# Attention outputs turned by VectorE and exchanged through DRAM instead of turned by TensorE, with other places for the adjacency loads

## The chip, the core and the metric

The kernel runs on one core of a Trainium2 chip. A core has five engines that each work through their own list of instructions in order: TensorE (PE; its weight loads are listed apart as PEld), VectorE (DVE), ScalarE (ACT), GpSimd (POOL) and SyncE (SP), which here only issues DMA transfers. An engine that meets an instruction whose semaphore is not yet up stands still, and so does all that is behind it in that list. The metric is the device time of one launch in microseconds (us), lower is better.

## The reference, cut to what matters

There are 16 graphs of 1024 nodes with 256 features, each with a symmetric 0/1 adjacency matrix with ones on its diagonal.

```python
h = relu(layernorm(x))
# layer 0: 8 heads of 32, queries = keys = values
normed = layernorm(h) * gamma1 + beta1
scores = einsum('bhqd,bhkd->bhqk', qkv, qkv) / sqrt(32)     # qkv: normed cut into heads
attn   = softmax(where(adj > 0, scores, -inf))
h      = h + einsum('bhqk,bhkd->bhqd', attn, qkv)
x      = x + h + gelu((layernorm(h)*gamma2 + beta2) @ W1 + b1) @ W2 + b2
# layer 1: one head over all 256 features
f = relu(layernorm(x)); hh = f @ W
e = leaky_relu(hh @ a_1 (per key and per query with a_2) + (hh @ a_12) @ hh.T, 0.2)
x = x + elu(f @ W_1 + softmax(where(adj > 0, e, -9e15)) @ f @ W_2)
```

All of it is float32. `adj` comes as int32, 4 MB for each graph. Because the queries of layer 0 are also its keys, the scores are symmetric, and so are the masked weights as long as `adj` is.

## The kernel before, in words

A graph (`b`, 0 to 15) is worked on in two halves, and two graphs are always in work at once: `attention(b)`, layer 0's attention of graph b, runs interleaved with `rest(b - 1)`, which is all that comes after the attention for the graph before it (the MLP with the groups `ph` and `po`, and layer 1 with `puT`, `pg`, `lg`, `pf`, `pa`).

**Order.** The program is written out by a small planner in Python, so that the order of instructions on every engine is fixed when the program is built. Six generators (`stream_a` for attention, `stream_b` for the rest, `stream_p` for the norms between them, `stream_c` for the prologue of the next graph, `stream_m` for the adjacency, `stream_s` for set-up) yield places on an axis on which graph b's attention covers b to b+1; the one with the lowest place goes next. A second clock counts estimated microseconds: `defer(us, f)` queues f until that clock has moved on by `us`. `turns` is a list of small TensorE transposes that `make_turns` puts between units. So a place such as b - 0.43 moves loads along the whole axis, and a `defer` of 2.0 instead of 3.0 moves one step by a fraction of a unit.

**Attention.** The heads are taken in groups of four (`g` = 0, 1), the queries in halves of 512 (`qh`), the keys in tiles of 128 (`kt`). A unit is one (qh, g, kt). It computes scores `s` on TensorE (line 1010), adds the mask on VectorE (L1023, `e<-s,mk`), takes Exp on ScalarE with the row sums (L1030), and one unit later multiplies with the values, `o<-e,va` (L1125), into one PSUM bank, the pool `pso` with a single buffer. From graph 1 on, symmetry is used: in the units with qh = 0, `keys` runs 4, 0, 5, 1, 6, 2, 7, 3, and for kt of 4 and more, `mirror` turns the weights in 32x32 blocks on VectorE (L1046), writes them to a DRAM scratch (`blocks`, L1053, four DMAs a unit) and adds up their columns on GpSimd (L1059, sent through `rows` and `gather`). In the second half (qh = 1) the lower key tiles are not computed again: `fetch(k)` loads them back from `blocks` into one half of the tile `em` (L1093), and `weigh_mirrored(k)` multiplies them (L1107), k from 0 to 15, two for each unit. Fetch k+2 may begin only when product k has been read. A graph thus has 16 units with qh = 0 and 8 with qh = 1.

**The end of a group.** When the last key tile of a (g, qh) is in, four groups a graph, `weigh` copies `o` (4 heads x 32 features on the partitions, 512 queries along them) to SBUF on VectorE (`os`, L1134). `close` puts `finish` into `turns`: four TensorE transposes to PSUM (`ptos`, L976) bring the queries onto the partitions, VectorE multiplies with the inverse row sums `rl` (`ot`, L978), and GpSimd adds the product to `h` (L982). `invert` makes `rl` from the row sums on VectorE. `prepare(b, st, c)` then takes layer norm statistics of `h` for chunk c of 256 rows; `rest` waits in its planning loop until `finished[b, 1]` is 2 before it prepares chunk 2.

**Adjacency.** `turn_masks(b, qh)` loads four tiles of 128 rows as int32 halves (`adj`, L587, two buffers), converts them on VectorE to fp8 (`mq`, L594, one buffer), and turns them with transposing DMAs into `mk` (L917, five buffers). `compare_masks` checks the symmetry: GpSimd subtracts `mk` and `mq` (`odd`, L932), and ScalarE sums the squares of the difference into a column of `uneven` (L941). If that or another condition fails at the end, a general path, not run here, computes everything again.

All bulk transfers go through SP's one list. Six lines show the two places where it meets the change:

```python
if n == NG * NT - 1:            # n counts the units of a graph, NG * NT = 16
    defer(2.0, lambda: fetch(0))
    defer(2.2, lambda: fetch(1))
...
if n == NG * NT + 1:
    gather(1)
```

Of the kernel before, what the change touches and what calls it, by code (L numbers as in the profile page):

```python
# [495 lines left out]
def fast_path(  # L496
# [427 lines left out]
    def compare_masks(b, qh, st):  # L924

        for half in range(qh + 1):
            for i in range(TPH):
                kt = qh * TPH + i
                odd = tmpp.tile([P, QW], BF16, tag="w1", bufs=6, name=f"odd_{b}_{qh}_{half}_{i}")
                key = st[half][:, kt // 2, :, kt % 2]  # L930
                query = st["mq", qh][:, i, half * QW : (half + 1) * QW]
                nc.gpsimd.tensor_tensor(  # L932
                    odd.rearrange("p (u v x) -> p u v x", u=2, v=2),
                    key.rearrange("p (u v x) -> p u v x", u=2, v=2),
                    query.rearrange("p (u x v) -> p u v x", u=2, v=2),
                    op=ALU.subtract,
                )
                n = (b * 3 + qh + half) * TPH + i
                defer(
                    3.0,  # L940
                    lambda odd=odd, n=n: nc.scalar.activation(odd, odd, AF.Square, accum_out=uneven[:, n : n + 1]),  # L941
                )
                yield
        if (b, qh) == (B - 1, NQH - 1):
            defer(
                4.0,
                lambda: nc.vector.tensor_reduce(
                    seen[:, 4:5], uneven, axis=mybir.AxisListType.X, op=ALU.add
                ),
            )  # L950
# [14 lines left out]
    scored = []  # L965

    finished = {}

    def finish(b, qh, g, rl, ready, os):
        h = hs[b]  # L970
        run_deferred(ready)
        finished[b, qh] = finished.get((b, qh), 0) + 1
        clock[0] += 0.5
        pt = ps_tile([P, TPH, P], f"ptos_{b}_{g}_{qh}")
        for t in range(TPH):
            nc.tensor.transpose(pt[:, t, :], os[:, t * P : (t + 1) * P], ident)  # L976
        ot = tmpp.tile([P, TPH, GH, HD], F32, tag="w2", bufs=4, name=f"ot_{b}_{g}_{qh}")
        nc.vector.tensor_mul(  # L978
            ot, pt.rearrange("p t (j d) -> p t j d", d=HD), rl.unsqueeze(3).to_broadcast([P, TPH, GH, HD])
        )  # L980
        ho = h[qh][:, :, g * P : (g + 1) * P]
        nc.gpsimd.tensor_add(ho, ho, ot.rearrange("p t j d -> p t (j d)"))  # L982

    def attention(b, st):
        va, kT = st["va"], st["kT"]
# [54 lines left out]
        def mirror(g, kt, es):  # L1040
# [17 lines left out]
            def add_up():  # L1058
                add = lambda out, p, q: nc.gpsimd.tensor_tensor(out, p, q, op=ALU.add)  # L1059
                part = denp.tile([P, TPH * GH, GH, 8], F32, tag="part", bufs=1, name=f"part_{b}_{g}_{kt}")  # L1060
                add(part, x[:, :, :, 0:8], x[:, :, :, 8:16])
                add(part, part, x[:, :, :, 16:24])
                add(part, part, x[:, :, :, 24:32])
                add(part[:, :, :, :4], part[:, :, :, :4], part[:, :, :, 4:])
                add(part[:, :, :, :2], part[:, :, :, :2], part[:, :, :, 2:4])
                row = denp.tile([P, GH, TPH, GH], F32, tag="row", name=f"row_{b}_{g}_{kt}")
                add(
                    row.rearrange("p a t h -> p t a h"),
                    part[:, :, :, 0].rearrange("p (t a) h -> p t a h", a=GH),
                    part[:, :, :, 1].rearrange("p (t a) h -> p t a h", a=GH),  # L1070
                )
# [48 lines left out]
        def weigh(qh, g, kt, es, first, last):  # L1120
            if first and not (mirrored and qh == 1):
                acc[g, qh] = pso.tile([P, QW], F32, tag="o", name=f"o_{b}_{g}_{qh}")
            o = acc[g, qh]
            for j in range(GH):
                nc.tensor.matmul(  # L1125
                    o[j * HD : (j + 1) * HD, :],
                    va[:, kt, (g * GH + j) * HD : (g * GH + j + 1) * HD],
                    es[j // 2][:, j % 2, :],
                    start=first and not (mirrored and qh == 1),
                    stop=last,  # L1130
                )
            if last:
                c = os[g, qh] = tmpp.tile([P, QW], F32, tag="w2", bufs=4, name=f"os_{b}_{g}_{qh}")
                nc.vector.tensor_copy(c, o)  # L1134
                if qh == NQH - 1:
                    close(qh, g)

        def close(qh, g):
            turns.append((1, lambda: finish(b, qh, g, *rl[g, qh], os[g, qh])))

        def invert(qh, g):
            r = smallp.tile([P, TPH, GH], F32, tag="rl", name=f"rl_{b}_{g}_{qh}")

            def f():
                if mirrored and qh == 0:
# [8 lines left out]
                )  # L1154
                nc.vector.reciprocal(r, r)

            rl[g, qh] = r, defer(2.5 if mirrored and qh == 0 else 2.5, f)

        keys = list(range(NT))
        if mirrored:  # L1160
# [5 lines left out]
        for n, u in enumerate(units):  # L1166
# [8 lines left out]
            if not mirrored:  # L1175
                if qh == NQH - 1 and kt % TPH == TPH - 1:
                    invert(kt // TPH, g)
                    if kt < NT - 1:
                        close(kt // TPH, g)
                yield 1.0  # L1180
                continue
            if qh == 0:
                if kt >= TPH:
                    mirror(g, kt, es)
                if n == NG * NT - 1:
                    defer(2.0, lambda: fetch(0))
                    defer(2.2, lambda: fetch(1))
                if n == NT + 1:
                    gather(0)
                if n == NT + 3:  # L1190
                    invert(0, 0)
                    close(0, 0)
                yield 1.0
                continue
            if n == NG * NT + 1:
                gather(1)
            if n == NG * NT + 3:
                invert(0, 1)
                close(0, 1)
# [46 lines left out]
    def rest(b, st, tails):  # L1246
# [476 lines left out]
```

## Time and profile before

| | |
|---|---|
| runs | 3390.57, 3390.76, 3401.56 us; median 3390.76 us |
| profiled execution | 3397.68 us; the profile's span in it 3395.4 us |
| mean granted TensorE clock | 0.988 of full |
| TensorE busy | 3239.8 us, 95% of the span |
| VectorE / ScalarE / GpSimd busy | 2584.0 (76%) / 2205.2 (65%) / 1515.3 us (45%) |
| `ptos` transposes, L976 | x256, 42.0 us |
| `os` copy, L1134; `ot` product, L978 | x64, 43.6 us; x64, 43.9 us |
| `odd` squares, L941 | x192, 119.9 us, with 37.0 us of accumulator reads |
| DMA through SP's queue | 397.14 MB, 48.0% of 16 engines' span |

A row of the groups names the line, the engine, the operation, the tile written and those read, the shape and the count; then the busy time and the mean of one, and after the bar the idle time of that engine just before such instructions with the names of those that ended it. A row of the waits says which engine and line waited for whom: us in total, times, the longest. A row of the windows gives, for a stretch of the span, busy us and instruction count of each engine, then the granted TensorE clock, the mean busy share of the DMA engines and GB/s. SPq is SP's list of issues.

### The profile page before, as it was taken

The page shows a single profiled execution, that of the slowest core. Times are in us where ns is not written, and L with a number is a line of the kernel's source. Part 1 is how long each engine was busy: PE and PEld are TensorE (multiplying, and loading weights), DVE is VectorE, ACT ScalarE, POOL GpSimd, SP SyncE. Part 2 cuts the span into 40 slices and gives each one's busy share as a digit, 9 for nine tenths or more (in the row PEclk, how much of TensorE's full clock was granted, in tenths as well). Part 3 has the DMA queues.
Part 4 walks back from the last instruction along what each step waited for, and adds up shares of the span by engine and source line. Part 5 has one row for each costly group of instructions (what it writes and reads, how often), then busy time and mean ns, then how long its engine had stood idle before and what let it go on. Part 6 is the DMA issues. An engine that isn't in the chain of part 4 may idle for free. (4 is left out here: it accounts for less than half of the span.)

```text
span 3395.4 us, 114970 instructions
## 1 busy us (share of the span) xinstructions
PE 3239.8 (95%) x48866; PEld 1600.2 (47%) x48866; DVE 2584.0 (76%) x4881; ACT 2205.2 (65%) x5384; POOL 1515.3 (45%) x1757
## 2 busy tenths in 40 slices
PE   6899999999999999999999999999999999999998
PEld 2244445444444444444444454444544444444477
DVE  5677787777888778787787887778877787877734
ACT  6875756758567585665757567585675856758553
POOL 3563543635436364453635436354362543636120
PEclk9999999999999999999999999999999999999999
DMA  5256454454654455555455544645445464444410
GB/s 136 69 112 141 114 134 128 102 150 116 141 131 109 131 120 133 132 119 128 109 147 123 135 121 110 150 115 136 126 104 141 114 144 127 109 130 113 119 36 14
DMA packets 741161, 404.82 MB, mean 119 GB/s; under 512 B 173217, under 2 KB 699937, under 8 KB 740641
## 3 DMA queue, kind: packets, MB, share of 16 engines
q1 hardware_dynamic: 740352, 397.14, 48.0%
q8 instruction: 386, 6.32, 0.8%
q14 instruction: 135, 1.10, 0.1%
q10 hardware_dynamic: 288, 0.26, 0.0%
HBM read 233.97 MB, written 146.54 MB: 112 GB/s over the span
## 5 line engine op out<-in xcount | busy, mean ns | idle before, releaser
L1030 ACT ACTIVATE e<-e 128x512 f32<-128x512 f32 x1504 | 929.5, 620 | 496.6 <-DVE e L1023 493.2
L1023 DVE TENSOR_TENSOR e<-s,mk 128x1024 f32<-128x1024 f32 x752 | 885.2, 1217 | 197.5 <-PE s L1010 182.8
L574 PE MATMUL lg<-fT,uT 128*32 128x256 f32 x7680 | 471.1, 392 | 0.0
L574 PE MATMUL ph<-yT,w 128*32 128x256 f32 x7808 | 443.3, 380 | 7.0 <-DVE yT L1292 7.0
L574 PE MATMUL pa<-gw,e 128*32 128x258 f32 x7584 | 446.1, 380 | 0.0
L1010 PE MATMUL s<-kT 32*64 32x512 f32 x6272 | 442.1, 614 | 0.9 <-DVE e L1023 0.9
L574 PE MATMUL po<-w,hid 128*32 128x256 f32 x7680 | 434.4, 379 | 0.0
L1125 PE MATMUL o<-e,va 128*32 128x512 f32 x3136 | 422.5, 606 | 0.4 <-ACT e L1030 0.4
L574 PEld LDWEIGHTS lg<-fT,uT 128*32 128x32 f32 x7680 | 255.8, 113 | 211.0 <-issue 48.4
L574 PEld LDWEIGHTS ph<-yT,w 128*32 128x32 f32 x7808 | 250.5, 110 | 210.4 <-issue 29.0
L1046 DVE STREAM_TRANSPOSE x<-e 128x1024 f32<-128x1024 f32 x240 | 293.7, 1239 | 73.0 <-ACT e L1030 44.4
L574 PEld LDWEIGHTS po<-w,hid 128*32 128x32 f32 x7680 | 250.0, 110 | 202.8 <-issue 45.2
L574 PEld LDWEIGHTS pa<-gw,e 128*32 128x32 f32 x7584 | 246.0, 110 | 185.5 <-issue 22.1
L1409 DVE SCALAR_TENSOR_TENSOR e<-lg,gw,mk 128x256 f32<-128x256 f32 x512 | 223.5, 478 | 125.9 <-PE lg L574 114.9
L1059 POOL TENSOR_TENSOR part<-part,x 128x512 f32<-128x512 f32 x240 | 310.3, 1293 | 18.8
L1415 ACT ACTIVATE e<-e,shift 128x512 f32<-128x512 f32 x256 | 183.5, 717 | 159.8 <-DVE e L1414 149.0
L1030 ACT ACTIVATION_READ_ACCUMULATOR e<-e 128x1 f32 x1504 | 283.4, 188 | 0.0
L1059 POOL TENSOR_TENSOR part<-x 128x512 f32<-128x512 f32 x120 | 156.5, 1304 | 230.4 <-DVE x L1046 224.6
L829 POOL TENSOR_TENSOR nrm<-nrm,g 128x256 f32<-128x256 f32 x128 | 110.8, 865 | 312.3 <-DVE nrm L749 312.3
L745 POOL TENSOR_TENSOR rs_c<-ve_c,mhalf 128x2 f32<-128x2 f32 x64 | 44.7, 699 | 421.0 <-DVE ve_c L743 421.0
L932 POOL TENSOR_TENSOR odd<-mk,mq 128x512 bf16<-128x512 fp8e5 x192 | 220.8, 1165 | 25.2 <-DMA mk<-mq 25.2
L1316 ACT ACTIVATE hid<-ph,b1c 128x256 f32<-128x256 f32 x512 | 204.9, 465 | 41.0 <-PE ph L574 26.5
(145 smaller groups left out, 4430.7 us busy)
## 6 DMA issues: line engine op xcount, KB each, us to landing
blocks<-x SPq DMA_DIRECT2D x480, 256.0 KB, 4.6
em<-blocks SPq DMA_DIRECT2D x240, 512.0 KB, 4.3
adj<-in_adj_dram SPq DMA_DIRECT2D x248, 256.0 KB, 4.0
h<-in_x_dram SPq DMA_DIRECT2D x64, 256.0 KB, 3.0
xb<-in_x_dram SPq DMA_DIRECT2D x128, 128.0 KB, 3.5
out_dram<-z SPq DMA_DIRECT2D x128, 128.0 KB, 4.0
rows<-row SPq DMA_DIRECT2D x120, 32.0 KB, 2.8
gather<-rows SPq DMA_DIRECT2D x120, 32.0 KB, 3.1
```

Source lines behind the costliest of these rows:

```text
L574: nc.tensor.matmul(out[c : c + HD], lhsT[:, c : c + HD], rhs, start=start, stop=stop)
L829: nc.gpsimd.tensor_mul(nrm, nrm, g1)
L932: nc.gpsimd.tensor_tensor(odd.rearrange("p (u v x) -> p u v x", u=2, v=2), key.rearrange("p (u v x) -> p u v x", u=2, v=2), query.rearrang ...
L1010: nc.tensor.matmul(sc[j // 2][c : c + P // 2, j % 2, :], kT[r, g, kt * P + c : kt * P + c + P // 2], kT[r, g, qs], start=j >= by_pe, stop= ...
L1023: nc.vector.tensor_tensor(e, masked, mb, op=ALU.add)
L1030: nc.scalar.activation(e[:, j], masked[:, j], AF.Exp, scale=SCALE, accum_out=sums[kt // TPH, g][:, n, kt % TPH, qh : qh + 1],)
L1046: nc.vector.transpose(x[:, :, 2 * i : 2 * i + 2, :].rearrange("p c h j -> p h c j"), es[i].rearrange("p h (c i) -> p h c i", i=HD),)
L1059: add = lambda out, p, q: nc.gpsimd.tensor_tensor(out, p, q, op=ALU.add)
L1125: nc.tensor.matmul(o[j * HD : (j + 1) * HD, :], va[:, kt, (g * GH + j) * HD : (g * GH + j + 1) * HD], es[j // 2][:, j % 2, :], start=first ...
L1316: nc.scalar.activation(hid[:, f0 + i, :], ph[:, i, :], AF.Identity, bias=b1c[:, f0 + i : f0 + i + 1])
L1409: nc.vector.scalar_tensor_tensor(e[:, j, :], lg[:, j, :], gw[:, kt, D : D + 1], st[c // 2][:, kt // 2, qs, kt % 2], op0=ALU.add, op1=ALU.add,)
L1415: ready = defer(2.5, lambda: nc.scalar.activation(e, e, AF.Exp, bias=shift))
```

## The change

1. The end of a group. `finish` is gone, and with it the four `ptos` transposes and `ot`. `weigh` now turns `o` straight out of PSUM with one VectorE transpose in 32x32 blocks (`xo`), which also takes the place of the copy `os`. What 32x32 blocks leave undone, the exchange of blocks between partition groups, is done by DMA: one write of 256 KB into a new DRAM scratch (`outs`, `defer(2.0)`), and four reads of 64 KB back into `os` (`defer(4.5)`).
2. `close` is a deferred step of 4.5 or 10.0: GpSimd multiplies `os` with `rl` and adds the product to `h`, two operations instead of one. The planning loop that waits for `finished` moves the clock when nothing else is left, which happens for the last graph alone.
3. The first two refills of `em` are deferred from unit 13 on instead of unit 15. The store of `rows` is deferred by 10.0 instead of 7.0.
4. For graphs 2 to 15, `turn_masks(b, 0)` starts at b - 0.73 instead of b - 0.43, with its comparisons behind it; `turn_masks(b, 1)` and its comparisons end at b + 0.26 instead of b + 0.36.
5. For qh = 1, two thirds of the comparisons, VectorE takes the largest absolute difference in place of ScalarE's sum of squares.

```diff
@@ compare_masks
-                defer(
-                    3.0,
-                    lambda odd=odd, n=n: nc.scalar.activation(odd, odd, AF.Square, accum_out=uneven[:, n : n + 1]),
-                )
+                def collect(odd=odd, n=n):
+                    if qh == 0:
+                        nc.scalar.activation(odd, odd, AF.Square, accum_out=uneven[:, n : n + 1])
+                    else:
+                        nc.vector.tensor_reduce(
+                            uneven[:, n : n + 1], odd, axis=mybir.AxisListType.X, op=ALU.max, apply_absolute_value=True
+                        )
+                defer(3.0, collect)
@@
-    def finish(b, qh, g, rl, ready, os):
-        h = hs[b]
-        run_deferred(ready)
-        finished[b, qh] = finished.get((b, qh), 0) + 1
-        clock[0] += 0.5
-        pt = ps_tile([P, TPH, P], f"ptos_{b}_{g}_{qh}")
-        for t in range(TPH):
-            nc.tensor.transpose(pt[:, t, :], os[:, t * P : (t + 1) * P], ident)
-        ot = tmpp.tile([P, TPH, GH, HD], F32, tag="w2", bufs=4, name=f"ot_{b}_{g}_{qh}")
-        nc.vector.tensor_mul(
-            ot, pt.rearrange("p t (j d) -> p t j d", d=HD), rl.unsqueeze(3).to_broadcast([P, TPH, GH, HD])
-        )
-        ho = h[qh][:, :, g * P : (g + 1) * P]
-        nc.gpsimd.tensor_add(ho, ho, ot.rearrange("p t j d -> p t (j d)"))
@@ mirror
-                defer(7.0, lambda: nc.sync.dma_start(blocks["rows", g][kt - TPH], row.rearrange("p a t h -> p (a t h)")))
+                defer(10.0, lambda: nc.sync.dma_start(blocks["rows", g][kt - TPH], row.rearrange("p a t h -> p (a t h)")))
@@ weigh
             if last:
-                c = os[g, qh] = tmpp.tile([P, QW], F32, tag="w2", bufs=4, name=f"os_{b}_{g}_{qh}")
-                nc.vector.tensor_copy(c, o)
+                turned = tmpp.tile([P, GH, TPH, HD], F32, tag="w2", bufs=4, name=f"xo_{b}_{g}_{qh}")
+                nc.vector.transpose(
+                    turned.rearrange("p a t d -> p t a d"), o.rearrange("p (t a i) -> p t a i", t=TPH, a=GH)
+                )
+                scratch = dramp.tile([P, GH, TPH * HD], F32, tag="outs", name=f"outs_{b}_{g}_{qh}")
+                c = os[g, qh] = tmpp.tile([P, GH, TPH, HD], F32, tag="w2", bufs=4, name=f"os_{b}_{g}_{qh}")
+                def exchange():
+                    for a in range(GH):
+                        nc.sync.dma_start(
+                            c[a * HD : (a + 1) * HD].rearrange("p j t d -> p j (t d)"),
+                            scratch[:, a].rearrange("(j i) e -> i j e", i=HD),
+                        )
+                defer(2.0, lambda: nc.sync.dma_start(scratch, turned.rearrange("p a t d -> p a (t d)")))
+                defer(4.5, exchange)
                 if qh == NQH - 1:
-                    close(qh, g)
-        def close(qh, g):
-            turns.append((1, lambda: finish(b, qh, g, *rl[g, qh], os[g, qh])))
+                    close(qh, g, 10.0)
+        def close(qh, g, us):
+            def f():
+                finished[b, qh] = finished.get((b, qh), 0) + 1
+                c = os[g, qh].rearrange("p j t d -> p t j d")
+                ho = hs[b][qh][:, :, g * P : (g + 1) * P].rearrange("p t (j d) -> p t j d", d=HD)
+                nc.gpsimd.tensor_mul(c, c, rl[g, qh].unsqueeze(3).to_broadcast([P, TPH, GH, HD]))
+                nc.gpsimd.tensor_add(ho, ho, c)
+            defer(us, f)
@@ attention
-                if n == NG * NT - 1:
+                if n == NG * NT - 3:
                     defer(2.0, lambda: fetch(0))
                     defer(2.2, lambda: fetch(1))
@@ rest
         while finished.get((b, 1), 0) < NG:
+            clock[0] += 0.5 if places[1] is None else 0.0
             yield 0.0, None
@@ stream_m
-                start, end = (b - 0.28, b - 0.10) if b == 1 else (b - 0.43, b - 0.25)
+                start, end = (b - 0.28, b - 0.10) if b == 1 else (b - 0.73, b - 0.60)
                 yield from spread(turn_masks(b, 0, states[b]), 5, start, end)
-                yield from spread(compare_masks(b, 0, states[b]), TPH, end + 0.01, end + 0.09)
-                yield from spread(turn_masks(b, 1, states[b]), 5, b + 0.03, b + 0.2)
-                yield from spread(compare_masks(b, 1, states[b]), 2 * TPH, b + 0.21, b + 0.36)
+                yield from spread(compare_masks(b, 0, states[b]), TPH, end + 0.01, end + 0.10)
+                yield from spread(turn_masks(b, 1, states[b]), 5, b + 0.02, b + 0.16)
+                yield from spread(compare_masks(b, 1, states[b]), 2 * TPH, b + 0.17, b + 0.26)
```

More of the change, by code (lines that the diff above doesn't have):

```diff
@@ L1132, in weigh @@
             if last:
-                c = os[g, qh] = tmpp.tile([P, QW], F32, tag="w2", bufs=4, name=f"os_{b}_{g}_{qh}")
-                nc.vector.tensor_copy(c, o)
-                if qh == NQH - 1:
-                    close(qh, g)
-        def close(qh, g):
-            turns.append((1, lambda: finish(b, qh, g, *rl[g, qh], os[g, qh])))
+                turned = tmpp.tile([P, GH, TPH, HD], F32, tag="w2", bufs=4, name=f"xo_{b}_{g}_{qh}")
[12 more added lines that the diff above has]
+                defer(4.5, exchange)
+                if qh == NQH - 1:
+                    close(qh, g, 10.0)
[7 more added lines that the diff above has]
+            defer(us, f)
         def invert(qh, g):
-            r = smallp.tile([P, TPH, GH], F32, tag="rl", name=f"rl_{b}_{g}_{qh}")
+            r = rl[g, qh] = smallp.tile([P, TPH, GH], F32, tag="rl", name=f"rl_{b}_{g}_{qh}")
             def f():
@@ L1155, in f @@
                 nc.vector.reciprocal(r, r)
-            rl[g, qh] = r, defer(2.5 if mirrored and qh == 0 else 2.5, f)
+            defer(2.5, f)
         keys = list(range(NT))
@@ L1178, in attention @@
                     if kt < NT - 1:
-                        close(kt // TPH, g)
+                        close(kt // TPH, g, 4.5)
                 yield 1.0
@@ L1191, in attention @@
                     invert(0, 0)
-                    close(0, 0)
+                    close(0, 0, 4.5)
                 yield 1.0
@@ L1198, in attention @@
                 invert(0, 1)
-                close(0, 1)
+                close(0, 1, 4.5)
             if last:
```

## The prediction

> **What bounds the kernel now.** I read the busy table first, then TensorE's waits, then one graph's stretch on three engines.
>
> ```profile
> span 3395.4 us, 114970 instructions
> PE 3239.8 (95%) x48866; PEld 1600.2 (47%) x48866; DVE 2584.0 (76%) x4881; ACT 2205.2 (65%) x5384; POOL 1515.3 (45%) x1757
> ```
>
> TensorE is the bound: 155.6 us of the span are not matmul, 15 us of these before the first one. So work taken off TensorE is worth its full time, and a new wait of TensorE costs its full time. TensorE's waits:
>
> ```profile
> PE o L1107 <- DMA em<-blocks: 64.5, 21, 5.2
> PE s L574 <- ACT e L1030: 14.6, 22, 1.6
> PE o L1107 <- DVE os L1134: 11.0, 12, 1.0
> ```
>
> The largest is the refill of `em`; the second lies in graph 0's attention alone. The groups concerned:
>
> ```profile
> L1107 PE MATMUL o<-em,va 128*32 128x256 f32 x1920 | 153.0, 391 | 78.4 <-DMA em<-blocks 64.5 <-DVE os L1134 11.0 <-DVE nrm L749 2.6
> L982 POOL TENSOR_TENSOR h<-h,ot 128x512 f32<-128x512 f32 x64 | 82.1, 1282 | 188.4 <-DVE ot L978 188.4
> L978 DVE TENSOR_TENSOR ot<-ptos,rl 128x512 f32<-128x512 f32 x64 | 43.9, 686 | 41.0 <-PE ptos L976 40.7
> L1134 DVE COPY os<-o 128x512 f32<-128x512 f32 x64 | 43.6, 682 | 0.0
> L976 PE MATMUL ptos<-ident,os 128*128 128x128 f32 x256 | 42.0, 286 | 1.1 <-DVE os L1134 1.1
> ```
>
> Where the `em` wait comes from is seen in graph 5, on SP's timeline and then on TensorE's (start, length, bracket: idle before):
>
> ```profile
> 1095.61 1.01 SPq L1093 DMA_DIRECT2D em<-blocks  x2
> ...
> 1108.40 0.81 SPq L587 DMA_DIRECT2D adj<-in_adj_dram  x2
> 1109.26 2.49 SPq L1084 DMA_DIRECT2D gather<-rows  x4
> 1111.85 1.51 SPq L1093 DMA_DIRECT2D em<-blocks  x2
> ```
>
> ```profile
> 1102.34 0.64 PE L1107 MATMUL o<-em,va 128*32 128x256 f32 x8 [0.93 <-DVE os L1134]
> 1109.60 0.61 PE L1107 MATMUL o<-em,va 128*32 128x256 f32 x8
> 1110.03 1.93 PE L574 MATMUL pa<-gw,e 128*32 128x258 f32 x32
> 1116.54 1.08 PE L1107 MATMUL o<-em,va 128*32 128x256 f32 x8 [4.58 <-DMA em<-blocks]
> 1117.39 3.64 PE L574 MATMUL lg<-fT,uT 128*32 128x256 f32 x32
> ```
>
> Refill k = 3 stands behind adjacency loads and `gather` in SP's list, is issued at 1111.85 and needed at 1111.96; TensorE stands for the landing (median 4.3 us). The next `lg` group takes 3.64 us where its like takes 1.91 at 1102.80: the clock fell. The windows name it (clock before the last two numbers):
>
> ```profile
> 1117.00:1121.00 4.00, 4.00 (x41) 1.58 (x33) 0.00 (x0) 0.00 (x0) 1.10 (x2) 0.50 0.81 196
> 1121.00:1125.00 4.00, 4.00 (x52) 1.84 (x52) 3.39 (x5) 1.09 (x2) 0.00 (x0) 0.87 0.11 36
> ```
>
> **What the Trainium skill says.** (1) "TensorE: Matmul & The Clock Gate", Part 1: a gate halves the clock after about one idle window of 3.4 us and gives it back after a busy one. The trace agrees: 0.50 after a wait of 4.58 us. (2) "DMA: Bandwidth & Descriptors", Anatomy of one DMA (told there for GpSimd's path): the DMA engines don't wait on semaphores, the issuing sequencer does, and most of a fixed 2.0 us is the receipt of the write. The trace agrees on the first (SP's list stands), and the smallest landing of `out_dram<-z`, also a write, is 1.7 us, its median 4.0. (3) "VectorE: DVE Perf Modes", The three transpose paths: VectorE turns 32x32 blocks only; hence the exchange. (4) "GPSIMD Engine Reference", 3.1: a two-input tensor operation is slowed by one read port; the trace has 1282 ns for 128x512.
>
> **The change part by part.** Sums are against the profiled execution (3397.68 us, span 3395.4), 0.2% over the median of 3390.76.
>
> *a. `ptos` leaves TensorE.* 256 transposes, 42.0 us in all, so 0.656 us a group. Three of the 64 groups lie in graph 0's attention, where TensorE waits for ScalarE anyway. 61 x 0.656 = **-40 us**. The built order keeps everything else on TensorE where it was, group by group, in all graphs, so nothing new takes the gap.
>
> *b. VectorE.* `os` (0.682) becomes the 32x32 transpose. PSUM as its source is not in the trace; the SBUF form has 1239 ns for 1024 columns, so about 0.62 for 512; bounds 0.6 and 1.24; I take 0.68, no difference. `ot` goes, -43.9 us. 128 comparisons come; the nearest row is the reduction of 128x512 at 0.644 us: +82 us. Net +38 on 2584, still 77%. Mean load hides it; placement decides. Half of the comparisons now wait on VectorE for GpSimd's `odd` (1165 ns each), where GpSimd has `part` sums of 5.4 us between them; behind a waiting comparison stand `e<-s,mk` and then Exp, and `weigh` needs these about 9 us after `s`. Worked on graph 6's trace, unit 5: `part` starts when `x` ends at 1217.5 and takes 5.4, the `h` and `xb` sums 1.5, the fourth `odd` 1.2: ready at 1225.6. VectorE gets there at 1221.0 + 0.6 + 0.4 + 0.6 = 1222.7, so it stands 3 us, and a later unit's Exp, with 2 to 3 us of slack, comes some 0.8 us late. The conversions of `mq`, moved to units 7 to 10, wait for `adj` landings (4.0 us) between short steps; 0 to 1.5 us each graph, but the same waits vanish from the second half (24.9 us before). Together **+12 us** (0.8 for each of 15 graphs), bounds 0 and +35.
>
> *c. ScalarE* loses 128 x (625 + 193 ns) = 105 us. It binds in graph 0's attention alone, where 8 of these lie: 6.5 us, of which I take **-5**.
>
> *d. GpSimd* gains 64 products of about 1.29 us, 83 us on 1515. Covered by its 55% of idle time; behind it are `rs` and the prologue's `va`, which have units of time. Without that cover the last group would cost its 2.6 us before `prepare`. For the last graph the way round (transpose, write, read, product, sum, norm: about 17 us) stands against 7 + 9 + 7 us of `ph`, `pa`, `ph`: nothing.
>
> *e. SP and `em`.* 320 issues and 33.5 MB more on 397 MB, 48% of the DMA engines' time to 52%. The order on SP for each graph now: `em` 0, 1 two units earlier; then `outs`, four `os`, `rows`, `em` 2, four `gather`, `em` 3. No adjacency loads stand between. At the first product VectorE comes about 1 us earlier (two conversions of 0.5 less in front), so the 0.93 us goes. Then, with W the landing of the 256 KB write and I one issue: write issued at 1101.4; `em` 2 lands at 1101.4 + W + 4I + 0.4 + 4.3; TensorE wants it at 1108.7, a wait of W + 4I - 2.6. `rows` lands 2.8 later, `gather` takes 4 x 0.48, so `em` 3 costs another 1.8. At the second exchange, four units on, `em` 10 stands behind it: W + 4I - 4.0. Neither W nor I is in the trace. W: 1.7 (shortest `out_dram`) to 4.6 (`blocks`, four in flight); I: 0.36 to 0.85. I take 2.7 and 0.45, as the queue is quiet there: W + 4I = 4.5, waits of 1.9, 1.8 and 0.5 = 4.2 us a graph, 63 us in 15. The row has 78.4 now: **-15 us**; bounds with the ends of W and I: -50 to +70.
>
> *f. The clock.* Waits of 3.1 us and more came in 14 graphs, and each brought a window or two at half rate, 1.7 us (half of 3.4) to 2.8 us (half of what 6.8 leaves after the wait) of lost work: some 30 us. In (e) no single wait reaches 3.4 us. I take **-22**; bounds 0 and -30.
>
> Sum: -40 + 12 - 5 - 15 - 22 = -70: span 3325, and 3391 - 70 = **3321 us**.
>
> **The rivals.** A change under 0.5% (17 us) is about what this measurement can't tell from none.
> *R1, the exchange blocks SP (slower).* If `outs` lands as `blocks` do (4.6) and an issue takes 0.85, W + 4I is 8.0: waits 5.4, 1.8, 4.0 = 11.2 us a graph, 168 against 78: +90, the clock falls as before, -40 + 12 - 5 + 90 = +57: 3448. With the clock lost it decides from W + 4I = 6.1 on (7.4 us a graph). For it: the median of `out_dram`. Against: the busy share of the DMA engines there was 0.88 to 0.92, half of it adjacency traffic that moves away.
> *R2, gain eaten by VectorE and SP.* Waits as long as now, VectorE at its bound: -40 + 35 - 5 = -10: 3381.
> *R3, the refills are simply in time.* Two units of lead and an exchange of 3 us: `em` waits of 1 to 2 us a graph: -40 + 5 - 5 - 52 - 30 = -122: 3269.
>
> **How the numbers follow.** Forecast (3290 to 3360) 0.55, R2 (3360 to 3407) 0.17, R1 0.18, R3 0.10. Faster: 0.55 + 0.10 + the part of R2 below 3374, 0.07 = 0.72; same 0.10; slower 0.18. The range leaves out about the lower half of R3 and the upper half of R1: 3275 to 3418. The forecast's own range is 3290 to 3360.
>
> **What would show it.** (a): no `ptos`; TensorE busy near 3198 plus or minus what the clock gives back. (e): the row `o<-em,va` idle near 63 us, in two pieces under 3.4 us, named DMA; R1 has over 110, R3 under 30. (f): a mean clock over 0.988. (b): `x<-` and `uneven` rows with waits for POOL `odd`; TensorE waits on ACT `e` in `o<-e,va`, 0.4 us now, near 12. I am wrong if a wait appears that no step names, above all TensorE behind `e<-e` or `ptk`, or if the transpose out of PSUM is far over 0.7 us.

## The result, and the profile after

The changed kernel takes 3514.2 us (median of 4 runs, 3503.6 to 3517.4), the kernel before beside it 3392.0 us (3390.6 to 3401.6). The ratio is 1.035, with an interval of 1.032 to 1.038: the change makes the kernel 122 us slower, where 70 us of gain were forecast. The profiled execution has a span of 3513.7 us.

The busy table of the kernel after:

```profile
span 3513.7 us, 114847 instructions
PE 3289.4 (94%) x48610; PEld 1613.1 (46%) x48610; DVE 2678.9 (76%) x4945; ACT 2123.3 (60%) x5128; POOL 1580.7 (45%) x1821
```

256 transposes of 42 us have left TensorE, and yet it is busy for 49.6 us more (3289.4 against 3239.8). Its idle time has grown too, from 155.6 to 224.3 us. Both have to be explained. TensorE's waits of the kernel after (us in total, times, longest):

```profile
PE o L1098 <- DMA em<-blocks: 63.8, 35, 3.4
PE ptf L1373 <- DVE mv_a L741: 44.8, 9, 5.0
PE ptf L1373 <- ACT ft L765: 21.3, 5, 4.5
PE ph L574 <- DVE yT L1304: 19.2, 49, 5.4
PE pty L1300 <- ACT hid L1328: 12.7, 14, 0.9
```

The `em` wait is 63.8 us, where 63 were forecast. `ptf`, with 7 us before, has 66: one wait of 4 to 5 us a graph, which no step of the prediction names. `ptf` turns the input of layer 1 and comes after `ft`, which ScalarE makes when VectorE has the statistics; both are late. The groups that answer to those of before:

```profile
L1098 PE MATMUL o<-em,va 128*32 128x256 f32 x1920 | 152.7, 391 | 63.8 <-DMA em<-blocks 63.8
L1125 DVE STREAM_TRANSPOSE xo<-o 128x512 f32<-128x512 f32 x64 | 44.9, 701 | 0.0
L944 DVE TENSOR_REDUCE uneven<-odd 128x1 f32<-128x512 bf16 x128 | 85.9, 673 | 70.4 <-POOL odd L932 70.4
L594 DVE TENSOR_SCALAR mq<-adj 128x512 fp8e5<-128x512 int32 x248 | 167.7, 696 | 146.1 <-DMA adj<-in_adj_dram 145.0
L1148 POOL TENSOR_TENSOR os<-os,rl 128x512 f32<-128x512 f32 x64 | 67.4, 1053 | 212.7 <-DMA os<-outs 154.8 <-DVE rl L1164 48.3 <-DVE rl L1167 9.6
L1149 POOL TENSOR_TENSOR h<-h,os 128x512 f32<-128x512 f32 x64 | 85.0, 1328 | 5.0
```

The durations of the new operations are close to those assumed or shorter (0.70 us for the transpose out of PSUM, where 0.68 was assumed; 0.67 for a comparison, 0.64 assumed; 1.05 for the product, 1.29 assumed). What is far off is idle time: VectorE stands 145.0 us for adjacency loads, against 24.9 before, and 70.4 us for `odd`.

The second-half exchange of graph 5, on SP's timeline and then on TensorE's:

```profile
1150.92 0.34 SPq L1138 DMA_DIRECT2D outs<-xo  x1
1152.96 2.41 SPq L1133 DMA_DIRECT2D os<-outs  x4
1155.46 0.38 SPq L1065 DMA_DIRECT2D rows<-row  x1
1155.94 0.38 SPq L1084 DMA_DIRECT2D em<-blocks  x1
1157.12 2.07 SPq L1075 DMA_DIRECT2D gather<-rows  x4
```

```profile
1160.68 1.08 PE L1098 MATMUL o<-em,va 128*32 128x256 f32 x8 [2.28 <-DMA em<-blocks]
```

This is the picture that step (e) of the prediction drew: the write, SP standing for its landing, four reads, `rows`, refill 2, and a wait of 2.28 us (1.9 forecast). But the clock falls here as well (clock 0.57 in the window of 4 us that begins just ahead of it):

```profile
1160.00:1164.00 4.00, 3.32 (x32) 1.58 (x36) 0.00 (x0) 0.13 (x1) 0.00 (x0) 0.57 0.80 193
```

Over the whole span, the trace's clock record has 150.2 us at half rate, in 29 stretches, against 84.5 us in 16 before.

**A wait that the table of waits doesn't show.** Two rows of TensorE's groups, before and then after:

```profile
L1010 PE MATMUL s<-kT 32*64 32x512 f32 x6272 | 442.1, 614 | 0.9 <-DVE e L1023 0.9
L1125 PE MATMUL o<-e,va 128*32 128x512 f32 x3136 | 422.5, 606 | 0.4 <-ACT e L1030 0.4
```

```profile
L1001 PE MATMUL s<-kT 32*64 32x512 f32 x6272 | 486.3, 634 | 3.8 <-DVE e L1014 3.8
L1116 PE MATMUL o<-e,va 128*32 128x512 f32 x3136 | 452.3, 620 | 0.0
```

The same instructions are busy for 44 and 30 us longer, with almost no idle time ahead. Where this comes from is seen on the timelines of one unit, TensorE's and VectorE's:

```profile
1289.38 1.92 PE L1001 MATMUL s<-kT 32*64 32x512 f32 x16
1291.22 1.06 PE L1116 MATMUL o<-e,va 128*32 128x512 f32 x7
1292.12 0.59 PE L1116 MATMUL o<-e,va 128*32 128x512 f32 x1
```

```profile
1275.86 0.69 DVE L944 TENSOR_REDUCE uneven<-odd 128x1 f32<-128x512 bf16 x1 [4.11 <-POOL odd L932]
1287.81 2.34 DVE L1014 TENSOR_TENSOR e<-s,mk 128x1024 f32<-128x1024 f32 x2
```

The sixteen `s` products of a unit take 1.11 us in the kernel before, here 1.92. They write two PSUM tiles, and each may be written again when VectorE has read it. The first of the two `e<-s,mk` here ends near 1289.0, the second at 1290.15; the trace has the first eight products starting by 1289.88 and the other eight from 1290.21 on. Half of the work runs, so TensorE counts as busy, while the other half waits for VectorE. In the same way `o` waits for the second Exp. Below, "late halves" means this. Counted from the trace, outside the stretches at half rate and after the first 230 us, such units lose 46 us in 85 places after, and nothing before. Why VectorE is late in this one unit is not shown by the lines: a comparison stood 4.11 us for `odd`, but that was 12 us earlier. Taken together, the late halves are not the comparisons' doing alone: by the same count they are 46 us in e2 below, which has the exchange and no comparison on VectorE, and some 20 us in w3, which has the comparisons and no exchange.

The difference of the spans, 118 us, is then: `ptos` -42; `em` -15; `ptf` +59; late halves of `s` and `o` +46; half rate +33 (half of 65.7); `ph` and `pty` +24; `pg` -8. That is +97; 21 us are not assigned. The +33 is an estimate: half rate is taken to lose half of its time.

### The profile page after: what moved, and what is told of

It is laid out like the page before. It is cut to its first block, busy times and chain, and to the rows that moved or that the text cites. A ratio compares the mean times of both kernels' runs of the same rounds, so it can differ in the third digit from the quotient of the medians.

```text
span 3513.7 us, 114847 instructions
## 1 busy us (share of the span) xinstructions
PE 3289.4 (94%) x48610; PEld 1613.1 (46%) x48610; DVE 2678.9 (76%) x4945; ACT 2123.3 (60%) x5128; POOL 1580.7 (45%) x1821
## 3 DMA queue, kind: packets, MB, share of 16 engines
q1 hardware_dynamic: 786432, 430.72, 48.7%
## 5 line engine op out<-in xcount | busy, mean ns | idle before, releaser
L1001 PE MATMUL s<-kT 32*64 32x512 f32 x6272 | 486.3, 634 | 3.8 <-DVE e L1014 3.8
L574 PE MATMUL ph<-yT,w 128*32 128x256 f32 x7808 | 456.8, 381 | 19.3 <-DVE yT L1304 19.2
L574 PE MATMUL pa<-gw,e 128*32 128x258 f32 x7584 | 460.0, 389 | 0.0
L1116 PE MATMUL o<-e,va 128*32 128x512 f32 x3136 | 452.3, 620 | 0.0
L574 PE MATMUL lg<-fT,uT 128*32 128x256 f32 x7680 | 450.2, 379 | 0.2 <-ACT gw L1403 0.2
L574 PEld LDWEIGHTS po<-w,hid 128*32 128x32 f32 x7680 | 282.0, 110 | 174.4 <-issue 41.7
L574 PEld LDWEIGHTS lg<-fT,uT 128*32 128x32 f32 x7680 | 247.9, 110 | 199.0 <-issue 27.2
L829 POOL TENSOR_TENSOR nrm<-nrm,g 128x256 f32<-128x256 f32 x128 | 101.0, 789 | 397.3 <-DVE nrm L749 397.3
L594 DVE TENSOR_SCALAR mq<-adj 128x512 fp8e5<-128x512 int32 x248 | 167.7, 696 | 146.1 <-DMA adj<-in_adj_dram 145.0
```

What stands on the lines that cost most here:

```text
L574: nc.tensor.matmul(out[c : c + HD], lhsT[:, c : c + HD], rhs, start=start, stop=stop)
L594: nc.vector.tensor_scalar(m[:, i * QW : (i + 1) * QW], a, 0.0, NEG8, op0=ALU.is_le, op1=ALU.mult, saturate=False)
L1001: nc.tensor.matmul(sc[j // 2][c : c + P // 2, j % 2, :], kT[r, g, kt * P + c : kt * P + c + P // 2], kT[r, g, qs], start=j >= by_pe, stop= ...
L1116: nc.tensor.matmul(o[j * HD : (j + 1) * HD, :], va[:, kt, (g * GH + j) * HD : (g * GH + j + 1) * HD], es[j // 2][:, j % 2, :], start=first ...
```

## The experiments

The first suspicion was the moved adjacency loads, since VectorE's largest new wait is for them (theory A); the rivals were the comparisons on VectorE (B) and the exchange in SP's list (C).

**Parts 4 and 5 undone, and part 4 alone.** e1 is the changed kernel with the places of before, e2 the changed kernel with all squares on ScalarE, e3 both; e4 is the kernel before with part 4 alone.

```diff
 e1, e3: stream_m as in the kernel before
-  (b - 0.73, b - 0.60)  ... (b + 0.02, b + 0.16) ... (b + 0.17, b + 0.26)
+  (b - 0.43, b - 0.25)  ... (b + 0.03, b + 0.2)  ... (b + 0.21, b + 0.36)
 e2, e3: collect
-  if qh == 0:
+  if True:              # sum of squares on ScalarE
 e4: kernel before, with the places of the changed kernel
```

> The changed kernel with part 4 undone: the adjacency loads, their conversions and the comparisons at the places of the kernel before. Theory A (VectorE stands for adjacency landings at the new places, 145 us, and hands that on to TensorE as ptf waits and half-rate clock): the mq row's idle falls under 40 us, the ptf waits under 15 us, the time to 3400-3440 us. Theory B (the comparisons on VectorE are the cause): 3490 us or more, ptf waits stay over 40 us. Theory C (the exchange in SP's list is the cause): 3480 us or more, with em waits near 64 us.

> The changed kernel with part 5 undone: all comparisons end in ScalarE's sum of squares again. Theory A: 3480-3505 us, since only the 70 us of uneven waits and about 1.3 us a graph of late score products go. Theory B: 3400-3440 us, ptf waits under 15 us although the mq row still idles some 140 us. Theory C: 3490 us or more.

> Parts 4 and 5 both undone: what is left is the exchange, its products on GpSimd and the earlier refills. Theories A and B, and A with B: 3320-3370 us, faster than the kernel before, because the four transposes a group have left TensorE (40 us). Theory C: 3450 us or more, em waits and waits for late h as in the changed kernel.

> The kernel before with part 4 alone (new places of loads and comparisons, squares on ScalarE, transposes on TensorE). Theory A: 3450-3500 us, ptf waits of 40 us and more. Theory B: 3385-3410 us. Theory C: 3375-3400 us, since without the exchange SP has room for the loads.

| kernel | us, median | ratio to before, 95% interval |
|---|---|---|
| changed | 3514.2 | 1.035 (1.032 to 1.038) |
| e1 places back | 3527.0 | 1.038 (1.037 to 1.040) |
| e2 squares back | 3484.5 | 1.026 (1.024 to 1.028) |
| e3 both back | 3470.2 | 1.023 (1.021 to 1.025) |
| e4 places alone | 3352.6 | 0.988 (0.986 to 0.990) |

Theory A falls: the new places alone make the kernel faster, by 44 us. TensorE's largest waits in e4:

```profile
PE ptf L1361 <- DVE mv_a L741: 22.4, 7, 4.3
PE ptk L837 <- POOL va L830: 20.0, 5, 15.9
PE ptf L1361 <- ACT ft L765: 18.7, 7, 3.7
```

No `em` wait is left: with the loads away, the refills are in time. VectorE stands 41.4 us for adjacency in e4 and 145.9 in e2 at the same places, so the long waits are made by the exchange. But e4 isn't free of VectorE's lateness either: its two `ptf` rows make 41.1 us, against 6.8 before, and this without any exchange. The comparisons (B) cost 30 us (e2 to the changed kernel) and 57 us (e3 to e1). Most of the cost is C: e3, all but the exchange and the refills undone, is still 2.3% slower than before, with an `em` wait of 106.0 us; and from e4 to e2 the exchange costs 132 us net of the transposes that it saves. As forecasts the ranges did less well: e2 (3484.5) fell into A's range and just under C's, and e4 is faster than all three allowed. A is excluded by e4; C rests on e3 and on the runs that follow. Beside the sets of runs told here the kernel before itself took 3392 to 3398 us, so differences between sets are good to a few us.

**What of the exchange costs.** All of the next four have the new places and the squares on ScalarE, as e2. x1 and x3 don't compute the reference: x1 leaves layer 0's attention out of `h`, x3 adds another group's numbers, scaled by 0.001. x1 has no exchange; x2 and x2b issue it from GpSimd's and from ScalarE's list; x3 leaves it in SP's, but its reads wait for no write.

```diff
 x1
-  outs write, four os reads
+  os[g, qh] = turned
-  nc.gpsimd.tensor_mul(c, c, rl[g, qh]...)
+  nc.gpsimd.tensor_mul(c, c, tiny...)          # zeros
 x2:  nc.sync.dma_start -> nc.gpsimd.dma_start  (write and reads)
 x2b: nc.sync.dma_start -> nc.scalar.dma_start
 x3
-  scratch[:, a].rearrange("(j i) e -> i j e", i=HD)
+  older[:, a].rearrange("(j i) e -> i j e", i=HD)   # the scratch of the group before; 0.001 for rl
```

> The changed kernel with the squares back on ScalarE, and without the exchange through DRAM: no outs write, no os reads; GpSimd multiplies the turned blocks where they lie, with zeros in place of rl, so layer 0's attention adds nothing to h. Everything else stays (transpose out of PSUM, two GpSimd operations a group, early refills, new places). Theory S (the five issues and the wait for the write in SP's one list make adjacency loads and refills late) and theory T (the 33.5 MB of traffic do): 3300-3345 us, em waits under 15 us. Theory R (the earlier refills and later rows, or the GpSimd products, are the cause): 3440 us or more.

> The changed kernel with the squares back on ScalarE, and the write and the four reads of the exchange issued from GpSimd's list in place of SP's; the traffic is the same. Theory S: 3320-3400 us, em waits under 25 us, if GpSimd can bear the issues. Theory T: 3460-3490 us, as with SP. Theory R: 3460 us or more.

> The same with the exchange issued from ScalarE's list: 320 issues of 0.33 to 0.45 us are some 130 us on ScalarE's 2202, and Exp stands where a write has not landed. Theory S: 3340-3420 us, em waits under 25 us. Theory T: 3460-3500 us. Theory R: 3460 us or more.

> The changed kernel with the squares back on ScalarE; the exchange stays in SP's list with all its issues and bytes, but the four reads take the scratch of the group before, long written, so SP never stands for a write to land (the numbers are then another group's, and the product is with 0.001 in place of rl). Theory S in the form that the wait is what costs: 3370-3430 us. S in the form that the issues cost: 3450-3480 us. Theory T: 3470-3490 us.

| kernel | us, median | ratio to before, 95% interval |
|---|---|---|
| x1 no exchange | 3310.5 | 0.974 (0.972 to 0.976) |
| x2 GpSimd's list | 3367.1 | 0.992 (0.990 to 0.994) |
| x2b ScalarE's list | 3405.3 | 1.002 (1.001 to 1.003) |
| x3 older scratch | 3399.1 | 1.001 (1.000 to 1.002) |

Without the exchange, everything else of parts 1 to 4 gives 3310.5 us: 42 us under e4, which is what the transposes were priced at. So the turn out of PSUM, GpSimd's two operations and the early refills together cost nothing that shows, and the exchange as it stands costs 3484.5 - 3310.5 = 174 us. Theory T, the traffic, can't be the main thing: the same bytes through GpSimd's list cost 57 us, and through ScalarE's 95. 85 of the 174 us go with SP's standing for the write (92.8 us in e2): x3 has the issues and the bytes, but no such wait. (Its product doesn't wait for `rl` either.)

A rival stands beside the list. With the list the DMA queue changes too: the profiles' tables of queues have the exchange in q1 with the loads in e2, in a queue q0 of its own in x2, and in q10 in x2b. No run keeps the queue and changes the list. But were q1 too full, the loads in it would land later, and they don't: from issue to landing an adjacency load takes 3.9 us in e2, 3.8 in x2 and x3 and 3.7 in x1 (medians). So the delay lies ahead of the issue.

What an issue in SP's list does to those behind it is seen in the first exchange of graph 5, which lies among the loads of graph 6. SP's timeline of x1, then of e2:

```profile
1012.04 0.89 SPq L587 DMA_DIRECT2D adj<-in_adj_dram  x2
1012.98 1.20 SPq L919 DMA_TRANSPOSE mk<-mq  x1
1017.99 0.82 SPq L587 DMA_DIRECT2D adj<-in_adj_dram  x2
1018.90 0.38 SPq L1067 DMA_DIRECT2D rows<-row  x1
1019.33 1.19 SPq L919 DMA_TRANSPOSE mk<-mq  x1
1022.23 1.75 SPq L587 DMA_DIRECT2D adj<-in_adj_dram  x2
```

```profile
1064.86 0.89 SPq L587 DMA_DIRECT2D adj<-in_adj_dram  x2
1069.56 0.33 SPq L1138 DMA_DIRECT2D outs<-xo  x1
1069.93 1.36 SPq L917 DMA_TRANSPOSE mk<-mq  x1
1071.40 1.15 SPq L587 DMA_DIRECT2D adj<-in_adj_dram  x2
1072.65 0.38 SPq L1065 DMA_DIRECT2D rows<-row  x1
1073.12 1.80 SPq L1133 DMA_DIRECT2D os<-outs  x4
1074.97 1.19 SPq L917 DMA_TRANSPOSE mk<-mq  x1
1076.99 1.48 SPq L587 DMA_DIRECT2D adj<-in_adj_dram  x2
```

In x1 the transposing DMA is gone 0.05 us after the loads ahead of it were issued. In e2 SP reaches `outs` first and stands until VectorE has turned `o` (it ends at 1069.53); the same DMA is then issued 4.2 us after those loads, and the next pair of loads behind it; then the four reads stand ahead of the next transposing DMA. The pair after that comes 10.2 us after the first in x1 (1012.04 to 1022.23), 12.1 us in e2. VectorE, in order as well, then stands for the landing (3.14 us at 1075.76 in e2, 0.70 at 1021.28 in x1), Exp behind it comes late, and so do `s`, `o`, `ft` and `ptf`. The order of these steps is read from the timelines of one exchange; that they make up the 174 us is argued. Between x1 and e2 the spans differ by 172 us: `em` waits 64, late halves of `s` and `o` 42 (46 against 4), half rate 29, `ptf` 16, `ph` 6, others 15.

The Trainium skill ("DMA: Bandwidth & Descriptors", Rules for kernel authors) says of spreading DMAs over several engines for the sake of bandwidth that "it only saves sequencer issue time". Here another engine's list is worth 117 us (e2 to x2). SP is no bound, so its 130 us of issuing (64 of 0.34 and 256 of some 0.43 us) would be worth nothing by themselves; what counts is what stands behind them and behind a waiting issue.

**Where the reads lie, and part 3.** x4 is e2 with part 3 undone; y1 is e2 with later reads; y2 is x2 with later reads; y3 has the write in SP's list and the later reads in GpSimd's.

```diff
 x4:  if n == NG * NT - 3: -> if n == NG * NT - 1:      rows: defer(10.0 -> defer(7.0
 y1, y2, y3:  defer(4.5, exchange) -> defer(9.0, exchange)   close(qh, g, 10.0) -> close(qh, g, 14.0)
 y2:  write and reads from nc.gpsimd;   y3: reads from nc.gpsimd
```

> The changed kernel with the squares back on ScalarE and part 3 undone: the first two refills are deferred from unit 15 again, rows by 7.0. Theory S (the exchange in SP's list is the whole cost): 3475-3500 us, since the early refills save at most the 15 us of two refills that don't wait. Rival: the early refills or the later rows make it worse: under 3465 us.

> The changed kernel with the squares back on ScalarE; the four reads are deferred by 9.0 instead of 4.5, the last group's product by 14.0 instead of 10.0, all in SP's list. The write has then landed before SP reaches the reads. If SP's standing for the write is the larger part of the cost: 3380-3420 us, as with the older scratch (3399), and no wait of SP for outs over 10 us in all. If it is the issues, or where the reads lie among the loads: 3450-3490 us.

> The exchange in GpSimd's list (squares on ScalarE) with the later reads: GpSimd stood 151 us for the write with reads at 4.5, and what is behind it there are the odd differences and the part sums. If that standing is what is left between 3367 and 3310: 3325-3350 us. If it is the issues on GpSimd (some 170 us) and the bytes: 3355-3375 us.

> The write in SP's list (64 issues that wait for nothing but VectorE), the reads in GpSimd's, deferred by 9.0 (squares on ScalarE). If only waits for landings hurt a list: 3320-3355 us. If SP's list suffers from any issue that is added: 3370-3420 us.

x4 took 3476.8 us (1.023, 1.021 to 1.025): part 3 brings nothing beside the exchange, if anything it costs a few us. y1 took 3437.0 us (1.012, 1.009 to 1.015). SP's wait for the write went from 92.8 to 15.9 us, but only 47 us of time were gained, where x3 gained 85; the reads now stand elsewhere in the list, and VectorE waits 40.3 us for `h` loads. So the wait is a large part, and the place of the four issues another. y2 took 3366.6 us (0.991, 0.989 to 0.993), as x2: GpSimd's own standing for the write (151 us, now 53) costs nothing. y3 took 3378.7 us (0.994, 0.992 to 0.996): the write alone in SP's list costs 12 us, and the reads there 58 more (y1), so it is the reads that hurt. This also prices the wait for VectorE that the timeline of e2 showed. SP stands for `xo` in y3 just as long as in e2, and pays 12 us for it with the issue. The rows of e2 and of y3:

```profile
SPq L1138 <- DVE xo L1125: 183.7, 18, 11.2
SPq L1138 <- DVE xo L1125: 180.6, 18, 11.5
```

y1 fell between the two ranges given for it. The others fell into one: x4 into that of the list as the whole cost, y2 into that of issues and bytes, y3 into that of any added issue.

**Issues or bytes, and the comparisons without the exchange.** w1 and w2 keep the number of issues and cut the bytes to a quarter; w3 is e4 with part 5; w4 is e4 with more room for the loads.

```diff
 w1, w2 (from x1): a write of turned[:, :, 0] and four reads of as much, from the scratch of the group before;
                   the product doesn't wait for them.  w1: nc.sync, defer(4.5);  w2: nc.gpsimd, defer(9.0)
 w3: kernel before + places of part 4 + collect of part 5
 w4: kernel before + places of part 4, but (b - 0.73, b - 0.60) -> (b - 0.73, b - 0.50)
```

> As without the exchange (3310), but SP issues one write and four reads a group again, each of a quarter of the bytes, with the reads from the scratch of the group before, so that SP stands for no write; GpSimd multiplies the turned blocks with zeros and waits for none of it. Against 3399 with all bytes and no wait: if the bytes are what is left, 3310-3345 us; if the issues in SP's list are, 3375-3400 us.

> The same quarter of the bytes issued from GpSimd's list with the later reads. Against 3367 with all bytes: if the bytes are what is left, 3310-3330 us; if GpSimd's 170 us of issues are, 3350-3370 us.

> The kernel before with parts 4 and 5 (new places, comparisons for qh = 1 on VectorE), no exchange. If the comparisons cost by themselves what they cost beside the exchange: 3380-3410 us, uneven waits near 70 us, late second halves of the score products. If they only hurt a VectorE that is already late: 3345-3362 us.

> The kernel before with part 4, where the loads and conversions of the first half are spread to b - 0.50 instead of b - 0.60. If the ptf waits that are left there (41 us) come from VectorE's conversions being packed: 3310-3340 us with ptf waits under 15 us. If they come from elsewhere, or the comparisons come too late behind: 3350-3400 us.

| kernel | us, median | ratio to before, 95% interval |
|---|---|---|
| w1 quarter of bytes, SP | 3410.9 | 1.004 (1.003 to 1.005) |
| w2 quarter of bytes, GpSimd | 3330.3 | 0.980 (0.978 to 0.982) |
| w3 places and comparisons | 3374.0 | 0.993 (0.991 to 0.995) |
| w4 places with more room | 3319.6 | 0.977 (0.975 to 0.978) |

In SP's list a quarter of the bytes costs 100 us and all of them 89 (x3). So the bytes are nothing there; the cost goes with the five places in the list, with no landing waited for. w1's smaller pieces make more packets, not fewer (811008 in q1; x3 has 786432, x1 740352), and an adjacency load lands after 3.8 us in w1 as in x3. In GpSimd's list a quarter of the bytes costs 20 us, and y2 36 more; whether these are bytes is not shown, since in y2 the product also waits for the reads and GpSimd for the write, and in w2 neither. As forecasts, w1 lies above both of its ranges, on the side of the issues, and w3 between its two. The comparisons cost 21 us by themselves (w3 against e4). w4 takes away the `ptf` wait that e4 had (0.5 of 41.1 us are left), and its mean clock is 0.997; it is 33 us faster than e4 and 2.3% faster than the kernel before.

**More room, with the exchange.** w5 is y2, w6 is e2, both with the first half's loads spread to b - 0.50.

```diff
-  (b - 0.73, b - 0.60)
+  (b - 0.73, b - 0.50)
```

> The exchange in GpSimd's list with the later reads, squares on ScalarE, and the loads of the first half spread to b - 0.50. If the 57 us left with GpSimd come from packed conversions that meet the traffic: 3285-3315 us, under the kernel with TensorE's transposes at the same places (3319.6). If they are issues and bytes whatever the places: 3330-3345 us.

> The exchange in SP's list as in the changed kernel, squares on ScalarE, the loads of the first half spread to b - 0.50. If the tight places hand the lateness on: 3330-3400 us. If SP's list is the cost by itself: 3440-3475 us, em waits near 60 us.

w6 took 3452.7 us (1.018, 1.016 to 1.020): 32 us better than e2, and room gained e4 as much (33). So the cost of SP's list doesn't come from tight places. TensorE's first two waits in w6 are those of the changed kernel still:

```profile
PE o L1098 <- DMA em<-blocks: 65.4, 41, 3.3
PE ptf L1373 <- ACT ft L765: 40.1, 14, 4.5
```

w5, which computes all of the reference, took 3316.4 us (0.977, 0.975 to 0.979), a little over the first of its two ranges, and can't be told from w4 (3319.6). With room for the loads and GpSimd's list, what the exchange costs and what TensorE's transposes cost are about the same. Both are faster than both kernels.

## Why the prediction was wrong

The runs split the change into four steps (medians): part 4 brings 44 us (before to e4); taking the transposes off TensorE brings 42 (e4 to x1); the exchange costs 174 (x1 to e2); the comparisons on VectorE cost 30 (e2 to the changed kernel). The second is what was forecast (-40); it is the exchange that turned the sign.

**(a) ptos, right.** -40 was forecast; x1 against e4 gives -42, and this holds the whole of parts 1 to 3 but the DMAs.

**(b) VectorE, wrong in a part.** The step gave the moved `mq` conversions 0 to 1.5 us a graph and took the waits of before (24.9 us) away in return. At the new places alone VectorE stands 41.4 us, and TensorE's `ptf` waits grow from 6.8 to 41.1 us (e4), 2.3 us a graph; more room takes them away, and 33 us of the time with them (w4). So a good part of the 66 us of `ptf` comes with the tight places and not with the exchange; part 4 gains all the same. With the exchange VectorE stands 145 us. The comparisons were given 0.8 us a graph by one late Exp; they cost 21 us alone and 30 beside the exchange, inside the bound of 35. A stand of 4.1 us for `odd` is there, where 3 were worked out on graph 6's trace. The sign named for it is not: TensorE's wait on Exp in `o<-e,va`, forecast near 12 us, doesn't stand in the table of waits, because such lateness hides in late halves.

**(c) ScalarE, -5, not shown.** In graph 0 the `s` wait for Exp stayed where it was (14.6 us before, 13.9 after).

**(d) GpSimd, right.** The products are hidden (x1 loses nothing by them), and between x2 and y2 GpSimd's standing for the write fell from 151 to 53 us without any gain.

**(e) SP and `em`: this step failed.** It was a sum over refills alone, and for two of the four exchanges a graph. "No adjacency loads stand between" was said of the second half. The first-half exchanges, which part 4 puts among the adjacency loads, their transposing DMAs and the next graph's `h` loads, were costed at nothing. What stands behind a waiting issue in SP's list was counted for one consumer of the list; the runs show that the rest, handed on by VectorE, costs more than the `em` waits themselves: 174 us in all, of which these are 64. The dear pieces are those of the four reads: 85 us go with their wait for the write (x3), and their issues cost too (58 us from y3 to y1, at the later places). The wait of `outs` for VectorE, also costed at nothing, is cheap (y3).

The sum for `em` agrees in its total, 63.8 us against 63, and in part by luck. The landing is 2.1 us and four issues some 1.8, so W + 4I is 3.9 (4.5 assumed), and with 3.9 the step's own formulas give 1.3 + 1.8 + 0 us a graph, some 46 us in 15. The waits also lie elsewhere than forecast: 34.2, 7.1 and 22.6 us at k = 2, 3 and 10, where 28, 27 and 8 were worked out. Its bounds, -50 to +70, don't follow from the ends of W and I that it names; these give -43 and, as in R1, +90. And the credit was wrong: part 4 alone would have taken all of the `em` idle time (e4), so -15 is -78 from part 4 and +64 from the exchange.

**(f) The clock, wrong.** "No single wait reaches 3.4" held for `em` (3.4 is the longest) and not for `ptf` (5.0), and a wait of 3.4 us isn't what decides: see the last section. The time at half rate nearly doubled, some +33 us of lost work where -22 were forecast.

**The signs.** The prediction named "a wait ... that no step names" as what would make it wrong, and `ptf` is that. TensorE's busy time was to be near 3198 and is 3289; 46 us of the difference are the late halves, which no wait shows, and some 33 come from more time at half rate. x1, without the exchange, has 3200. The Trainium skill ("Perfetto Trace Analysis", Identifying the Most-Contended Engine) says that matmul busy time is no good measure of how near TensorE is to its limit. The trace agrees, for another reason than the page gives (instructions that overlap): 46 us of waiting lie in it.

**The rivals.** R1 had the sign and the list, but let it decide through `em` from W + 4I = 6.1 on. At 3.9 the exchange already cost 174 us, most of it through the other loads. R2 and R3 didn't occur; refills simply in time, as in R3, are what e4 and x1 have, without the exchange.

What stays open: how the 89 to 100 us of places in SP's list split over the four exchanges of a graph and between issue time and order; what part of GpSimd's 57 us is bytes; and 21 us of the difference of the spans.

## What to carry to other kernels

A DMA that is issued from a list shared with loads costs what it makes late for everything behind it: its waits, then its issues. Here the wait for an earlier transfer was dear and the wait for an engine's result was not. Go through the whole list, for every place where the step occurs, and not through the consumer that one has in mind. A round trip through DRAM belongs in the list of an engine whose standing costs nothing; here that was GpSimd, and it was worth 117 us. And try the parts of a change one by one: in this one, a part that only moves loads carries a gain, and it was hidden behind the others.

## What was not expected of the hardware

- **The clock falls after a window that is half idle.** The clock record changes on a grid of 3.41 us. In the twenty traces of this case (364 falls), every such window that was followed by a fall held between 1.65 and 3.41 us of TensorE idle time, and none with more than 2.01 us was followed by full rate; between 1.65 and 2.01 both occur. A wait of 2.3 us, as in the exchange shown above, is therefore enough when it lies within one window. The prediction had looked for waits over 3.1 us. The Trainium skill ("TensorE: Matmul & The Clock Gate", Part 1) has the free-running window of 3413 ns, which these traces confirm, and speaks of an idle one; here an idle half of it or a little more suffices.
- **Row-tiled products can be half stopped.** Eight score products that wait for their PSUM tile leave the other eight running alone, at 1.92 us for the sixteen instead of 1.11, without a gap on the timeline.
- **The issue list decides, not the bytes.** With the reads in SP's list at 4.5 and no landing to wait for, a quarter of the bytes took as long as all of them (3411 and 3399 us), and the same quarter in GpSimd's list 3330 us.
